# A decoder layer with a Mamba-2 mixer: B and C of a group in a turn of their own, by seven block products, and two products of out_proj over two turns

## The chip, the core and the metric

The kernel runs on one core of a Trainium2 chip. A core has a matrix engine (PE, with the loading of weights into its array shown as PEld), a vector engine (DVE), a scalar engine (ACT), GpSimd (POOL) and a sync engine (SP), which here issues the DMAs. The engines run side by side and each works through its own queue in order; they wait for one another by semaphores. All data of this kernel are fp32, and a matmul appears in the trace as two passes. The metric is the device time of one execution in microseconds, lower is better. Before the change it is 869.28 us, the median of three runs (869.14 to 869.52).

## The reference

The layer takes `x`, two batches of 256 tokens of width 512, through three residual blocks, each after a layer norm: a Mamba-2 mixer, a product with a context that is rounded to 8 bits (fake quantisation), and a feed-forward with soft-selected low-rank experts. The mixer takes nearly all of the time:

```python
proj = h @ in_proj_w.T                      # 512 -> 8192 gate + 8192 hidden + 1024 B + 1024 C + 128 dt
hBC  = silu(causal_conv(hBC, conv_w, conv_b))       # four taps along the tokens, per channel
hid, B, C = split(hBC)                      # 128 heads of 64; 8 groups, each with one B and one C of 128
M      = einsum('bcihn,bcjhn->bcijh', C, B) * L     # L: decays between tokens of a chunk of 128
Y_diag = einsum('bcijh,bcjhp->bcihp', M, hid * dt)
Y_off  = ...                                # what the second chunk takes over from the first
y   = Y_diag + Y_off + D * hid
yg  = y * silu(gate)
ygr = yg * rsqrt(mean(yg * yg over the 1024 channels of a group) + eps)
out = (ygr * gnorm_w) @ out_proj_w.T        # 8192 -> 512
```

## The kernel before

The tokens of both batches lie side by side, T = 512 columns; S = 256 is one batch. `hT` holds the normed input, 512 channels as KD = 4 blocks of 128 partitions, 512 tokens. The 8192 hidden channels make 64 *tiles* of 128, and NG = 8 *groups* of GJ = 8 tiles. A tile needs 128 rows of `in_proj_w` for the hidden part and 128 for the gate.

**Seven products for eight.** The first nine tiles are projected plainly (`project`, L304): for hidden and gate four matmuls of 512 columns each, 8 in all. From tile 9 on the two row blocks (hidden, gate) and the two halves of the 512 input channels make a 2 x 2 block matrix, which meets the 2 x 2 blocks of `hT` (halves of the channels, batches). Seven products of two matmuls of 256 columns (`multiply`, L308), 14 in all, replace the plain eight of 512. For this POOL makes four sums of weights per tile (`sum_weights`, L358, tile `ws`; those of the input, `hs`, are made once). The first four products are in `begin` (L370), three more in `complete` (L399); DVE makes the sums between them (`sum_begun`, L389: L395 to L397; `sum_complete`, L406: L410, L411), with a first copy by ACT (L387). The result lies in the two PSUM banks of `xy`, of which there are two sets. The gate comes out negated, one batch of it in the SBUF tile `u`.

**B and C of a group** are projected plainly: `project_b` (L438) writes the PSUM bank `po` and `project_c` (L441) the bank `misc` (for group 1, `po`), four matmuls of 512 columns each (16 passes together). Each then gets the convolution (`Conv`, L315): the first tap on ACT (L322), three more on DVE (L329), SiLU on ACT (L340).

**A turn** of the main loop (L965) handles tile c = 8 g + j, and at the same time tile c-1 (convolution, gate, decays) and tile c-2 (the products of the state space). The queues of PE, DVE, ACT and POOL hold the instructions in just the order in which they are written; SP's order is set by a planner. On PE a turn is: `begin` of tile c; a product of out_proj; `heads` of tile c-2 (L511, bank `py`); in turn j = 3 the B of the next group; four transposes of tile c-1 (`by_tokens`, L477, `pht` in the bank `misc`, read by DVE into `hc`, L486); `complete` of tile c; in turn 3 the C of the next group (in group 0, C of group 1 in turn 4). In turn 6 and 7 the small products of B and C (`pcb`, `pcr`) stand behind `begin`.
On DVE a turn is: `sum_complete` of tile c-1 (which waits for PE's last product of the turn before); at times the end of a group's norm; in turn 1 of four groups the rounding of a block of the context (L281, L282); the first scan of decays (L498); the three taps; `sum_begun` of tile c; the second scan; the sums of out_proj; the gating of tile c-2 (L530, L533); `hc` of tile c-1. On POOL: the four weight sums of the next tile, the product of decays and B-C for each scan (L508, `mT`), the sums for out_proj, and the running sum of squares (L539, `sqsum`).

**out_proj of a group** runs while the next group is projected, again as seven block products, m1, m2, m6, m5, m7, m3, m4 in this order (`seventh`, L656), each eight matmuls (16 passes) into the one bank `po`. They stand in turns 1, 2, 4, 5, 6, 7 of the next group and turn 0 of the one after; turn 3 has none, since it holds B and C. The sums that these need are made on POOL (L592 to L623: s1 and s3 of a pair of tiles, s2, s4, and t1 to t4 of the weights `wo`). m2 is followed by the group's norm (`norm`, L542): `pss` on PE from `sqsum`, `var` on DVE, a power on POOL (`r_g`), and at the head of the next turn on DVE four small operations for the reciprocal root and two adds into `acc` (L652), which free `po`. The last group but one uses the order 1, 2, 5, 6, 7, 3, 4 in turns 1 to 7, and the last group a plain out_proj at the end.

Tile c+1's weights (two DMAs of 256 KB) and decays (two of 384 KB) are loaded in turn c; `wo` (two of 1 MB per group) in turn 1 by the program, earlier by the planner, into three buffers.

Of the kernel before, what the change touches and what calls it, by code (L numbers as in the profile page):

```python
# [54 lines left out]
def kernel(  # L55
# [34 lines left out]
    loaded = []  # L90

    def load_w(*rows, name):

        w = wpool.tile([P, 2, KD, P], F32, tag="w", name=name)
        if rows[1] == rows[0] + 1:
            ins = nc.sync.dma_start(out=w[:], in_=in_w[rows[0] : rows[0] + 2].rearrange("r p k o -> p r k o"))
        else:
            for n, r in enumerate(rows):
                ins = nc.sync.dma_start(out=w[:, n], in_=in_w[r])
        loaded.append(ins)  # L100
        return w

# [14 lines left out]
    cb = const.tile([P, 80], F32, name="cb")  # L117
    gw = const.tile([P, NG * GJ], F32, name="gw")
# [196 lines left out]
    class Conv:  # L315
# [3 lines left out]
        def __init__(self, dst, pv, c, name):  # L319
            self.dst, self.pv, self.c = dst, pv, c  # L320
            self.a = pool.tile([P, T], F32, tag="conv", name=f"conv_{name}")
            nc.scalar.activation(  # L322
                by_batch(self.a[:]), pv, AF.Identity, bias=cb[:, c : c + 1], scale=cw[:, c, 3:4]
            )

        def taps(self):
            av, pv, c = by_batch(self.a[:]), self.pv, self.c
            for d in range(1, 4):
                nc.vector.scalar_tensor_tensor(  # L329
                    av[:, :, d:],  # L330
                    pv[:, :, : S - d],
                    cw[:, c, 3 - d : 4 - d],
                    av[:, :, d:],
                    ALU.mult,
                    ALU.add,
                )

        def finish(self):
            self.taps()
            nc.scalar.activation(self.dst, self.a[:], AF.Silu)  # L340

    class Tile:


        def __init__(self, c):
            self.c, self.plain = c, c <= GJ
            self.lT, self.mT = [], []

    def load_tile(c):
        z = Tile(c)  # L350

        z.w = wpool.tile([P, 2, KD, P], F32, tag="w", name=f"w_{c}")
        for n, r in enumerate((HID0 + c, GATE0 + c)):
            loaded.append(nc.sync.dma_start(out=z.w[:, n], in_=in_w[r]))
        z.dec = load_decays(c)
        return z

    def sum_weights(z):  # L358
        if not z.plain:
            a11, a12, a21, a22 = (z.w[:, r, h, :] for r in range(2) for h in (lo, hi))  # L360
            s = pool.tile([P, 3, KD // 2, P], F32, tag="ws", name=f"ws_{z.c}")
# [8 lines left out]
    def begin(z):  # L370

        z.xy = ps_proj.tile([P, 2, T], F32, tag="xy", name=f"xy_{z.c}")
        if z.plain:
            for n in range(2):
                project(z.xy[:, n, :], z.w[:, n])
            return
        z.halves = [z.xy[:, n, half] for n in range(2) for half in (slice(0, S), slice(S, T))]
# [6 lines left out]
    def copy_first(z):  # L384
        if not z.plain:
            z.u = pool.tile([P, 2, S], F32, tag="u", name=f"u_{z.c}")
            nc.scalar.copy(z.u[:, 0], z.halves[0])  # L387

    def sum_begun(z):  # L389
        if not z.plain:  # L390
            z.v = pool.tile([P, 2, S], F32, tag="v", name=f"v_{z.c}", bufs=1)
            _, x1, _, y1 = z.halves
            u0, u1 = z.u[:, 0], z.u[:, 1]
            y = z.xy[:, 1, :].rearrange("p (n s) -> p n s", n=2)
# [11 lines left out]
    def sum_complete(z):  # L406
        if not z.plain:
            x1 = z.halves[1]
            y = z.xy[:, 1, :].rearrange("p (n s) -> p n s", n=2)
            nc.vector.tensor_tensor(x1, x1, z.u[:, 0], ALU.add)  # L410
            nc.vector.tensor_tensor(y, y, z.v[:], ALU.add)  # L411

    def start_conv(z):
        z.hid = pool.tile([P, T], F32, tag="hid", name=f"hid_{z.c}", bufs=2)
        flat = z.xy[:].rearrange("p n s -> p (n s)")
        z.conv = Conv(z.hid[:], by_batch(flat[:, 0:T] if z.plain else flat[:, S : S + T]), z.c, f"h_{z.c}")

    def gates(z, half):
# [6 lines left out]
        elif half == 0:  # L425
            nc.scalar.activation(z.gate[:], z.xy[:, 1, :], AF.Silu)  # L426

    def load_bc(g):
        return load_w(B0 + g, C0 + g, name=f"wbc_{g}")

# [752 lines left out]
```

## Time and profile before

| | us |
|---|---|
| median of three runs | 869.28 (869.14 to 869.52) |
| the profiled execution | 869.89 |
| its span, first to last instruction | 867.0 |
| from the start of c in group 1 to that in group 2 | 98.87 |
| granted PE clock, mean over the span | 0.997 |

The page gives busy time per engine over the span. Matmul ends are modelled, so PE's share says little alone; the *chain* does more: it goes back from the last instruction, at each step to what released it, and lists start, length and engine with the line. A row of the *timeline* has start, length, engine, line, operation, output and inputs, shapes, count, and in brackets the idle time before it with what ended it. A row of the *windows* has the stretch, its length, then the busy time of PE, PEld, DVE, ACT and POOL (with counts), the PE clock, the DMA share and GB/s. Line numbers with L are those of the kernel before.

### The profile page before, as it was taken

What the parts mean: (1) busy time and instruction counts of PE and PEld (TensorE: products, weight loads), DVE (VectorE), ACT (ScalarE), POOL (GpSimd) and SP (SyncE); (2) the same over time, 40 slices, a digit from 0 to 9 for tenths busy, and PEclk for the clock granted to TensorE, in tenths of its full rate; (3) what the DMA queues carried; (4) which work ended last, traced back from release to release, by engine and by line L of the source; (5) the groups of instructions that cost most, each with busy time, mean ns of one, the idle gap of its engine ahead of it and who ended that gap; (6) DMA issues with size and microseconds to landing.
All of it is one profiled execution on the core that took longest, in us unless ns stands there. A gap on an engine that the chain in (4) does not pass through costs nothing.

```text
span 867.0 us, 12832 instructions
## 1 busy us (share of the span) xinstructions
PE 855.9 (99%) x4360; PEld 641.8 (74%) x4360; DVE 719.0 (83%) x1133; ACT 360.5 (42%) x779; POOL 631.2 (73%) x614
## 2 busy tenths in 40 slices
PE   8999999999999999999999999999999999999998
PEld 6444586888868886888868887788868888885453
DVE  5668798998898998988899888988799888995663
ACT  2444554444444443444444443444444443443220
POOL 2146798987799778987889778997789878973210
PEclk9999999999999999999999999999999999999998
DMA  6774453336433383336533362435333363323001
GB/s 171 221 268 146 140 169 114 112 109 225 141 106 131 109 254 117 106 120 203 169 105 122 104 219 89 133 108 177 140 119 112 111 209 104 122 86 122 0 1 48
DMA packets 54418, 116.19 MB, mean 134 GB/s; under 512 B 7217, under 2 KB 7473, under 8 KB 54354
## 3 DMA queue, kind: packets, MB, share of 16 engines
q1 hardware_dynamic: 54354, 115.39, 40.4%
q8 instruction: 34, 0.56, 0.3%
q14 instruction: 30, 0.25, 0.1%
HBM read 111.83 MB, written 3.54 MB: 133 GB/s over the span
## 4 chain that ended last, share of the span: by engine, by line
PE 85%; DVE 10%; DMA 1%; issue 1%; POOL 1%; ACT 1%; SPq 0%; ACTq 0%; POOLq 0%; DVEq 0%
PE xy L310 32%; PE m L643 18%; PE py L518 9%; PE xy L306 7%; PE pht L482 4%; PE c L306 3%; PE po L701 3%; DVE conv_h L329 2%; DVE lT L498 2%; PE pf L809 2%; PE pq L809 2%; PE pcb L451 1%; PE b L306 1%; DVE acc L652 1%; DMA wo<-in_out_w 1%
## 5 line engine op out<-in xcount | busy, mean ns | idle before, releaser
L508 POOL TENSOR_TENSOR mT<-lT,inner 128x768 f32<-128x768 f32 x128 | 233.4, 1824 | 128.6 <-ACT lT L502 115.6
L498 DVE TENSOR_TENSOR_SCAN lT<-dec,seed 128x512 f32<-128x512 f32 x128 | 154.9, 1211 | 0.0
L329 DVE SCALAR_TENSOR_TENSOR conv_h<-xy,cw,conv_h 128x510 f32<-128x510 f32 (+2 forms) x192 | 143.0, 745 | 13.7 <-ACT gate L426 5.5
L643 PE MATMUL m<-wo,yw 128*128 128x256 f32 x672 | 151.9, 379 | 0.0
L643 PEld LDWEIGHTS m<-wo,yw 128*128 128x128 f32 x672 | 126.8, 190 | 16.7
L502 ACT ACTIVATE lT<-dec,lT 128x128 f32<-128x128 f32 x256 | 88.8, 395 | 116.5 <-DVE lT L498 95.0
L310 PE MATMUL xy<-hT,w 128*128 128x256 f32 x440 | 113.8, 381 | 0.3
L310 PE MATMUL xy<-hs,w 128*128 128x256 f32 x440 | 112.9, 379 | 0.0
L310 PE MATMUL xy<-hs,ws 128*128 128x256 f32 x440 | 103.9, 379 | 0.0
L518 PE MATMUL py<-mT,hc 128*64 128x256 f32 (+1 forms) x1024 | 97.3, 332 | 0.0
L539 POOL TENSOR_TENSOR sqsum<-sqsum,sq 128x512 f32<-128x512 f32 x56 | 72.3, 1291 | 31.6 <-ACT sq L538 27.5
L518 PEld LDWEIGHTS py<-mT,hc 128*64 128x64 f32 x1024 | 63.4, 136 | 40.1 <-issue 16.1
L310 PEld LDWEIGHTS xy<-hs,w 128*128 128x128 f32 x440 | 83.6, 190 | 11.4
L310 PEld LDWEIGHTS xy<-hs,ws 128*128 128x128 f32 x440 | 83.6, 190 | 11.4
L310 PEld LDWEIGHTS xy<-hT,w 128*128 128x128 f32 x440 | 79.2, 190 | 13.0 <-DVE u L397 1.9
L538 ACT ACTIVATE sq<-y 128x512 f32<-128x512 f32 x56 | 35.3, 631 | 101.6 <-DVE y L533 97.3
L322 ACT ACTIVATE conv_h<-xy,cb,cw 128x512 f32<-128x512 f32 x64 | 49.6, 775 | 57.4 <-DVE xy L411 56.7
L530 DVE SCALAR_TENSOR_TENSOR py<-hid,dsk,py 128x512 f32<-128x512 f32 x64 | 47.8, 747 | 25.8 <-PE py L518 25.8
L306 PE MATMUL xy<-hT,w 128*128 128x512 f32 x144 | 63.3, 592 | 0.0
L310 PE MATMUL xy<-hT,ws 128*128 128x256 f32 x220 | 56.5, 379 | 0.0
L340 ACT ACTIVATE hid<-conv_h 128x512 f32<-128x512 f32 x64 | 40.4, 631 | 31.3 <-DVE conv_h L329 31.2
L410 DVE TENSOR_TENSOR xy<-xy,u 128x256 f32<-128x256 f32 x55 | 23.7, 431 | 35.3 <-PE xy L310 35.3
(205 smaller groups left out, 1341.6 us busy)
## 6 DMA issues: line engine op xcount, KB each, us to landing
dec<-decays SPq DMA_DIRECT2D x128, 384.0 KB, 3.4
w<-in_in_w SPq DMA_DIRECT2D x128, 256.0 KB, 3.1
wo<-in_out_w SPq DMA_DIRECT2D x16, 1024.0 KB, 8.0
wbc<-in_in_w SPq DMA_DIRECT2D x16, 256.0 KB, 3.9
kvin<-in_ctx_kv SPq DMA_DIRECT2D x4, 512.0 KB, 3.5
kvq<-kvin SPq DMA_DIRECT2D x4, 512.0 KB, 4.5
kv<-kvq SPq DMA_DIRECT2D x4, 512.0 KB, 3.6
acc<-in_x SPq DMA_DIRECT2D x4, 256.0 KB, 3.6
```

The source lines that it names most:

```text
L306: nc.tensor.matmul(pp, w[:, k, :], hT[:, k, :], start=(k == 0), stop=(k == KD - 1))
L310: nc.tensor.matmul(out, w[:, k, :], h[:, k, :], start=(k == 0), stop=(k == KD // 2 - 1))
L322: nc.scalar.activation(by_batch(self.a[:]), pv, AF.Identity, bias=cb[:, c : c + 1], scale=cw[:, c, 3:4])
L329: nc.vector.scalar_tensor_tensor(av[:, :, d:], pv[:, :, : S - d], cw[:, c, 3 - d : 4 - d], av[:, :, d:], ALU.mult, ALU.add,)
L340: nc.scalar.activation(self.dst, self.a[:], AF.Silu)
L498: nc.vector.tensor_tensor_scan(lT[:, 0:NT, :].rearrange("p t i -> p (t i)"), dec[:, 0:T], seed[:], 0.0, ALU.mult, ALU.add)
L502: nc.scalar.mul(lT[:, NT + b, :], dec[:, T + b * P : T + (b + 1) * P], lT[:, 2 * b, P - 1 : P])
L508: nc.gpsimd.tensor_tensor(m[:], z.lT[n][:], inner[:], ALU.mult)
L518: nc.tensor.matmul(z.py[n * HD : (n + 1) * HD, b * S + s * P : (b + 1) * S], z.hc[:, 2 * b + s, n, :], z.mT[n][:, part, :], start=(s == 0) ...
L530: nc.vector.scalar_tensor_tensor(py[:], hid[:], dsk[:, c : c + 1], py[:], ALU.mult, ALU.add)
L539: nc.gpsimd.tensor_tensor(sqsum[:], sqsum[:], sq[:], ALU.add)
L643: nc.tensor.matmul(o.po[:, t, :], lhs[k][:, t * P : (t + 1) * P], rhs[k], start=(k == 0), stop=(k == GJ // 2 - 1))
```

## The change

A group now has nine turns. Turn 4 (`BC`) belongs to the B and C of the next group, as a `State` that passes through the same functions as a tile: `load`, `sum_weights`, `begin`, `sum_begun`, `complete`, `sum_complete`. From group 2 on it is projected by the seven products, so C comes out negated, half of it in `u`: its convolution takes negated weights (`ncw`, made once) and runs in two halves (`parts`), 6 DVE taps of 256 columns in place of 3 of 512. A State has no decays, scans, `mT`, `heads`, gating or transposes. B and C of group 0 stay plain in the first turn, B now in `misc` and C in `po`; those of group 1 stay plain, B in `xy` and C in `po`. The last group keeps eight turns.

The products of out_proj stand at turns 1, 2, 4, 5, 6, 7, 8. `block` became a generator that may stop between its two halves (8 passes each): m2 runs in turns 2 and 3, m4 in turn 8 and turn 0 of the next group. The norm's `pss`, `var` and power stand ahead of the product in turn 2, its end and the adds of m2 at the head of turn 4. In the last group all products run whole, in turns 1, 2, 3, 5, 6, 7, 8. `pcb` and `pcr` stand at turns 7 and 8, ACT's copies of them ahead of the turn's decays.

```diff
@@ -316,49 +304,49 @@
-        def __init__(self, dst, pv, c, name):
-            self.dst, self.pv, self.c = dst, pv, c
+        def __init__(self, dst, pvs, w, c, name):
+            self.dst, self.w = dst, w
             self.a = pool.tile([P, T], F32, tag="conv", name=f"conv_{name}")
-            nc.scalar.activation(
-                by_batch(self.a[:]), pv, AF.Identity, bias=cb[:, c : c + 1], scale=cw[:, c, 3:4]
-            )
-        def taps(self):
-            av, pv, c = by_batch(self.a[:]), self.pv, self.c
+            av, n = by_batch(self.a[:]), NB // len(pvs)
+            self.parts = [(av[:, i * n : (i + 1) * n], pv) for i, pv in enumerate(pvs)]
+            for a, pv in self.parts:
+                nc.scalar.activation(a, pv, AF.Identity, bias=cb[:, c : c + 1], scale=w[:, 3:4])
+        def finish(self):
             for d in range(1, 4):
-                nc.vector.scalar_tensor_tensor(
-                    av[:, :, d:],
-                    pv[:, :, : S - d],
-                    cw[:, c, 3 - d : 4 - d],
-                    av[:, :, d:],
-                    ALU.mult,
-                    ALU.add,
-                )
-        def finish(self):
-            self.taps()
+                for a, pv in self.parts:
+                    nc.vector.scalar_tensor_tensor(
+                        a[:, :, d:], pv[:, :, : S - d], self.w[:, 3 - d : 4 - d], a[:, :, d:], ALU.mult, ALU.add
+                    )
             nc.scalar.activation(self.dst, self.a[:], AF.Silu)
...
+            self.c, self.name, self.plain = c, f"{c}", c <= GJ
+            self.rows = HID0 + c, GATE0 + c
             self.lT, self.mT = [], []
-    def load_tile(c):
-        z = Tile(c)
-        z.w = wpool.tile([P, 2, KD, P], F32, tag="w", name=f"w_{c}")
-        for n, r in enumerate((HID0 + c, GATE0 + c)):
-            loaded.append(nc.sync.dma_start(out=z.w[:, n], in_=in_w[r]))
-        z.dec = load_decays(c)
-        return z
+    class State:
+        def __init__(self, g):
+            self.g, self.name, self.plain = g, f"bc_{g}", g <= 1
+            self.rows = B0 + g, C0 + g
+    def load(z):
+        z.w = wpool.tile([P, 2, KD, P], F32, tag="w", name=f"w_{z.name}")
+        for n, r in enumerate(z.rows):
+            nc.sync.dma_start(out=z.w[:, n], in_=in_w[r])
+        if isinstance(z, Tile):
+            z.dec = load_decays(z.c)
...
+        if isinstance(z, State) and z.plain:
+            c = ps_out.tile([P, T], F32, tag="po", name=f"c_{z.g}")
+            if z.g == 0:
+                b = ps_misc.tile([P, T], F32, tag="misc", name="b_0")
+                z.xy = [b[:], c[:]]
+            else:
+                xy = ps_proj.tile([P, 2, T], F32, tag="xy", name=f"b_{z.g}")
+                z.xy = [xy[:, 0, :], c[:]]
+        else:
+            xy = ps_proj.tile([P, 2, T], F32, tag="xy", name=f"xy_{z.name}")
+            z.xy = [xy[:, n, :] for n in range(2)]
+            z.flat = xy[:].rearrange("p n s -> p (n s)")
         if z.plain:
             for n in range(2):
-                project(z.xy[:, n, :], z.w[:, n])
+                project(z.xy[n], z.w[:, n])
             return
...
+    def hid_of(z):
+        return by_batch(z.xy[0] if z.plain else z.flat[:, S : S + T])
     def start_conv(z):
-        z.hid = pool.tile([P, T], F32, tag="hid", name=f"hid_{z.c}", bufs=2)
-        flat = z.xy[:].rearrange("p n s -> p (n s)")
-        z.conv = Conv(z.hid[:], by_batch(flat[:, 0:T] if z.plain else flat[:, S : S + T]), z.c, f"h_{z.c}")
+        if isinstance(z, Tile):
+            z.hid = pool.tile([P, T], F32, tag="hid", name=f"hid_{z.c}", bufs=2)
+            z.convs = [Conv(z.hid[:], [hid_of(z)], cw[:, z.c], z.c, f"h_{z.c}")]
+            return
+        g = z.g
+        z.sT = [pool.tile([P, T], F32, tag=f"{n}T", name=f"{n}T_{g}", bufs=1) for n in "bc"]
+        z.convs = [Conv(z.sT[0][:], [hid_of(z)], cw[:, 64 + g], 64 + g, f"b_{g}")]
+        if z.plain:
+            pvs, w = [by_batch(z.xy[1])], cw[:, 72 + g]
+        else:
+            pvs, w = [a.unsqueeze(1) for a in (z.halves[3], z.u[:, 1])], ncw[:, g]
+        z.convs.append(Conv(z.sT[1][:], pvs, w, 72 + g, f"c_{g}"))
...
-    turns_of_sums = [usual_sums] * (NG - 1)
-    def block(o, lhs, rhs, name):
+    last_sums = {n + (n >= 4): of for n, of in usual_sums.items()}
+    turns_of_sums = [usual_sums] * (NG - 2) + [last_sums]
+    def block(o, lhs, rhs, name, split):
         o.po = ps_out.tile([P, 2, S], F32, tag="po", name=f"{name}_{o.g}")
         for t in range(2):
+            if t == split:
+                yield
...
-    def seventh(o, m):
+    def seventh(o, m, split):
         sub, add = ALU.subtract, ALU.add
         early = o.g == NG - 2
+        split = 1 if split else None
         if m == 0:
-            block(o, left(o, 0, 0), right(o, 0, 0), "m1")
+            yield from block(o, left(o, 0, 0), right(o, 0, 0), "m1", split)
             o.u = pool.tile([P, 2, S], F32, tag="ou", name=f"ou_{o.g}", bufs=1)
             nc.scalar.copy(o.u[:], o.po[:])
         elif m == 1:
-            block(o, left(o, 0, 1), right(o, 1, 0), "m2")
-            middle, end = norm(o)
+            yield from block(o, left(o, 0, 1), right(o, 1, 0), "m2", split)
             nc.vector.tensor_tensor(o.po[:], o.po[:], o.u[:], add)
-            middle()
-            return lambda: (end(), add_block(o, 0, 0))
+            ends_of.append(lambda: (o.end_norm(), add_block(o, 0, 0)))
         elif m == 2:
...
-    usual = {1: 0, 2: 1, 4: 2, 5: 3, 6: 4, 7: 5, 8: 6}
-    turns = [usual] * (NG - 2) + [{1: 0, 2: 1, 3: 3, 4: 2, 5: 4, 6: 5, 7: 6}]
+    GT = GJ + 1
+    BC = GJ // 2
+    order = []
+    for g in range(NG):
+        for q in range(GT):
+            if q != BC:
+                order.append((g, q, Tile(g * GJ + q - (q > BC))))
+            elif g + 1 < NG:
+                order.append((g, q, State(g + 1)))
+    order += [(NG, q, None) for q in range(2)]
+    usual = {1: (0, 0), 2: (1, 1), 4: (2, 0), 5: (3, 0), 6: (4, 0), 7: (5, 0), 8: (6, 1)}
+    turns = [usual] * (NG - 2) + [{1: (0, 0), 2: (1, 0), 3: (3, 0), 5: (2, 0), 6: (4, 0), 7: (5, 0), 8: (6, 0)}]
+    going = []
     inner = {}
-    NTILE = NG * GJ
     last_o = outs[NG - 1]
+    def products_of_state(g, q):
+        if g < NG and q == GT - 2:
+            inner[g] = inside(g, *state.sT)
+        if g < NG and q == GT - 1:
+            between(g, *state.sT, inner[g], (ps_misc, "misc"))
...
+    for s, (g, q, z) in enumerate(order):
+        z1, z2 = (order[s - n][2] if s >= n else None for n in (1, 2))
+        tile1 = isinstance(z1, Tile)
+        c = g * GJ + q - (q > BC) if q != BC or g == NG else None
         if z:
             begin(z)
-        if c + 1 < NTILE:
-            tiles.append(load_tile(c + 1))
-            sum_weights(tiles[c + 1])
+        if order[min(s + 1, len(order) - 1)][2]:
+            load(order[s + 1][2])
+            sum_weights(order[s + 1][2])
...
+        if g > 0:
+            products_of_state(g + 1, q)
...
+        if q == 2 and 0 < g < NG:
+            middle, outs[g - 1].end_norm = norm(outs[g - 1])
+            middle()
...
+        if z1 and not tile1:
+            z1.convs[1].finish()
+            state = z1
+        for o, turn in ((outs[g] if g < NG else None, q - GT), (outs[g - 1], q)):
             if o and 0 <= o.g <= g and not o.plain:
                 for stage, n in turns_of_sums[o.g].get(turn, ()):
                     stage(o, n)
...
-        for o, turn in ((outs[g - 1], j), (outs[g - 2], j + GJ)):
-            if 0 <= o.g < g and not o.plain and turn in turns[o.g]:
-                ends_of.append(seventh(o, turns[o.g][turn]))
...
+        o = outs[g - 1]
+        if not going and 0 <= o.g < g and not o.plain and q in turns[o.g]:
+            going.append(seventh(o, *turns[o.g][q]))
+        if going and next(going[0], True):
+            going.pop()
...
+        if s == 0:
+            begin(state)
+            start_conv(state)
+            state.convs[0].finish()
```

## The prediction

> **What bounds the kernel now.** I read four views: the page's busy line, whole groups by windows, the chain, and PE's own timeline where the chain leaves PE. The busy line:
>
> ```profile
> PE 855.9 (99%) x4360; PEld 641.8 (74%) x4360; DVE 719.0 (83%) x1133; ACT 360.5 (42%) x779; POOL 631.2 (73%) x614
> ```
>
> PE's 99% is modelled and proves little; that the others are clearly below it is to be seen. Next, two whole groups (window, its length, then busy us of PE, PEld, DVE, ACT, POOL), cut at the start of `c`:
>
> ```profile
> 146.06:244.93 98.87, 98.46 (x533) 79.62 (x533) 88.11 (x132) 44.00 (x98) 82.87 (x82) 1.00 0.44 144
> ...
> 541.40:640.27 98.87, 98.46 (x532) 79.62 (x533) 86.38 (x130) 42.76 (x97) 82.19 (x82) 1.00 0.40 133
> ```
>
> The first holds the rounding of a context block, the second doesn't: DVE works 1.7 us less and the length stays. The chain in two stretches (start, us, what):
>
> ```profile
> 639.62 0.61 DVE hc L486
> 640.23 0.04 issue
> 640.27 3.70 PE c L306 x8
> 643.97 3.45 PE xy L310 x16
> 647.42 3.45 PE m L643 x16
> 650.88 1.48 PE py L518 x16
> 652.35 0.11 issue
> 652.46 0.63 PE pht L482 x4
> 653.09 6.04 PE xy L310 x28
> ...
> 724.44 2.61 PE xy L310 x12
> 727.05 0.02 issue
> 727.07 0.44 DVE xy L410
> ...
> 730.21 0.89 DVE acc L652 x2
> 731.10 0.14 issue
> 731.23 3.69 PE m L643 x16
> ```
>
> PE follows PE, except before `c` and, in the last group, before one out_proj product (731.23). PE's timeline of turn 3, where b and c lie:
>
> ```profile
> 236.21 1.52 PE L518 MATMUL py<-mT,hc 128*64 128x256 f32 x16
> 237.66 3.70 PE L306 MATMUL b<-hT,wbc 128*128 128x512 f32 x8
> 241.20 0.60 PE L482 MATMUL pht<-ident,hid 128*128 128x128 f32 x4
> 241.82 1.13 PE L310 MATMUL xy<-hT,w 128*128 128x256 f32 x4
> ...
> 244.93 1.55 PE L306 MATMUL c<-hT,wbc 128*128 128x512 f32 x3 [0.25 <-DVE hc L486]
> ```
>
> PE pieces of one group by the chain: eight tiles of 6.04 (28 passes of 256 columns, 0.2157 each), eight py of 1.45, eight pht of 0.59, seven out_proj products of 3.45, pcb 0.89, pcr 0.45, pss 0.79 and b with c, 16 passes of 512 columns. Such 16 take 6.87 where nothing interrupts (the plain tiles), 0.4294 each. Sum 97.85. The chain's period is 98.84 (541.43 to 640.27): 1.0 us per group is PE waiting, nearly all around b and c. So a steady group is bound by PE, with 10 us of room on DVE and 16 on POOL; only order within a turn can make PE wait.
>
> **The change, part by part.** Times below count from PE's start of a turn.
>
> *Block products.* The B and C of groups 2 to 7 go from 16 passes of 0.4294 (6.87) to 28 of 0.2157 (6.04): -0.83 in six groups, -5.0. Groups 0 and 1 stay plain. All of it is on the path.
>
> *Own turn.* With b and c gone from turn 3, the waits at 241.20 (for hid), 241.82 (for L397), 244.93 (the misc bank, still read by hc) and 652.35 have no instruction to hold: up to -1.0 in six groups. Bounds 0 to -6.0; I take -6.0, as the split turns below keep more distance.
>
> *The split products.* They cost PE nothing. They make turns of 9.8 (0), 11.5 (1), 10.6 (2), 9.8 (3), 11.5 (4, the states), 10.9 (5), 10.1 (6), 12.4 (7) and 10.3 (8). But m2 now ends in turn 3, so its rstd and add come at the head of turn 4 on DVE, and m6 of that turn needs the one `po` bank that this add frees. Before, turn 3 had the rstd and no product. The last group shows the very sequence: from 727.07 rstd and add end at 731.10, and the product that could start at 727.05 + 3.45 = 730.50 starts at 731.23. That is a new wait of 0.73, plus DVE's lateness at the start of turn 4. Bounds: 0.73, and 1.1 with DVE 0.4 late; I take 0.85, six times, +5.1. Behind it on PE wait m6, py, pht and the rest of the turn; DVE uses the time to finish that turn's sums, so nothing else is late.
>
> *DVE.* A tile's turn takes DVE 9.2 (turn 0 of the second group, 197.27: L486 issues at 207.58 and frees DVE 0.6 later, less 0.2 at the start and 1.5 for m4's adds). The state adds L395 to L397 (1.5) and L410, L411 (1.1) and six half taps for three whole ones. A half tap isn't in the trace: between 0.44 (L652, 256 columns, 24.5 us over 56) and 0.745 (L329 whole); I take 0.44, nearer in size. Turn 4 also gets rstd and add (2.9, 233.94 to 236.84) and m6's sum (0.65); turn 5 has neither scans nor hc, but a wait of 0.8 for ACT's first tap. Turns 0 to 8 by DVE: 10.7, 9.2, 9.3, 9.9, 12.7, 10.2, 10.0, 10.7, 9.2, sum 91.9 against PE's 97.0. sum_begun ends 6.2 after L410, and PE asks for it at 7.2 in half-product turns, 8.9 in full ones. So turn 0 hands on 0.9 of lateness, which turn 1 absorbs unless the rounding (1.94, 210.08 to 212.02) lies there: 0.2 + 0.9 + 1.9 + 6.2 = 9.2 against 8.95, +0.25 in groups 2 to 4, +0.75. (In group 1, turn 0 holds a plain tile and no product.) With taps of 0.745 turn 6 would begin 1.7 late and wait 0.5, +3 in all.
>
> *POOL.* Four weight sums more per group (0.73 each, L364 to L367), +2.9. The heavy pair is turns 2 and 3: 25 us of work in 20.4. By the rows of 221.88 to 247.6 laid end to end from 1.5 into turn 2: weight sums 2.95, mT 1.8, r_g 1.2, s1 and s3 1.5, t1 2.45, mT 1.75; then 2.95, 1.8, s2 2.75, t2 2.45, done at 23.4. m6 asks for the last at 20.4 + 3.45 + 0.86 = 24.7, and 0.85 later with its wait. 2.1 to spare: cost nothing; this cover is the first rival. pss moves ahead of m2, to 3.45 in turn 2, and waits for sqsum, which POOL frees at 1.5 (221.88 against 220.34): nothing.
>
> *ACT, queues.* ACT has some 50 us free per group; its pieces for C (256 columns, 0.37 to 0.48) stand before the taps as a gate's do now. SP: state weights are the same 16 loads, without decays, so that turn loads less. The wo load that m4 releases issues 6.3 into turn 0 (203.54) and would issue at 4.6; with the row's median landing of 8.0 it is there at 12.6, asked for at 14.1; at the worst landing, 9.8, 0.3 late. Nothing, as now.
>
> *Unchanged:* prologue, group 0, last group from turn 1, tail.
>
> *Sum:* -5.0 - 6.0 + 5.1 + 0.75 = -5.1. The profiled execution took 869.89, 0.6 above the median of 869.28; -5.1 gives 864.8 against it, **864.2** against the median.
>
> **Two rules weighed.** *A DVE operation with two SBUF inputs:* three of C's six taps read the SBUF half (u) and accumulate in SBUF. The one such row, L675, took 742 ns against 666 for L673 beside it, while the POOL pair L619 took 2.95 against 2.5: by it, +0.2 on DVE and up to +1.4 on POOL per group, in turn 5 where both have it; nothing on PE. The Trainium skill, "SBUF — State Buffer", section "Who interferes with whom", says that such an instruction contends with GpSimd reading SBUF, and that the one that issues first blocks the other. Taken fully, each of the three would sit out a POOL sum of 0.73, 2.2 per group on DVE, and PE would wait some 0.9 in turn 6, six times: about 869.5 as an estimate. This rule speaks against the change; L675 shows a tenth of it.
>
> *PE's headroom:* PE pieces adjoin in the chain although weight loads are busy 74%. The window without rounding is as long as the one with it, on 1.7 us less DVE. The Trainium skill, "Perfetto Trace Analysis", section "Identifying the Most-Contended Engine", judges PE by its arithmetic and the weight loads' busy share, not by matmul busy time; by the 74% PE would have room and DVE, at 83%, would be the engine to relieve, so that 0.83 less on PE would give nothing and 3.0 more on DVE would cost up to 18 in six groups. The window contradicts it here.
>
> **The rivals.**
> *Slower: POOL late for m6.* For: the pair of turns holds more POOL work than PE time, with no b and c to stretch turn 3 as now. Against: POOL even idles 2.2 before its mT of turn 3 now (238.86). Each us beyond the 2.1 costs six. It ends slower once POOL is 3 us later than laid out; at 3.5, 864.2 + 6 x 1.4 = 872.6.
> *No gain: DVE is late around the states.* C's half taps take 0.745 and PE waits 0.5 in turn 6 (867.2), or half a clash with POOL as in L282 (2182 ns once, 1098 else) comes on top and it waits 1.0 (870.2). For: DVE is fullest in turn 4. Against: no half-sized DVE row takes over 0.48.
> *More gain: m6 doesn't wait,* because DVE starts the sums earlier than PE needs the bank: 864.2 - 5.1 = 859.1. Against: the group-7 lines, where DVE started at once and it waited all the same.
>
> **How the numbers follow.** Forecast 0.68 (862 to 867.5, its own bounds: m6 at 0.73 and no late turn 1 below, half of the old waits staying above); DVE late 0.13; POOL late 0.12; m6 free 0.07. 0.2% is 1.7 us, about what a measurement can tell from no change. Faster (below 867.5): the forecast, m6 free and a third of "DVE late", 0.79; within 0.2%: the rest of it, 0.08, rounded down for a late turn elsewhere; slower: POOL late and that, 0.13. The range, 860 to 869.5, holds the forecast and most of "DVE late", not POOL late and little of m6 free.
>
> **What would show it.** b and c gone and new 28-pass groups in the chain at 0.2157; a period of 97.9 per group (98.2 with rounding); one PE wait per group of 0.7 to 1.1 before the product of turn 4, released by DVE's add; half taps of 0.44 spacing; POOL's t2 done before that product. Wrong if PE waits for POOL there, for L397 in turns 0, 1, 3 or 6, or if the period stays at 98.8.

## The result, and the profile after

The changed kernel takes 892.73 us (median of five, 892.03 to 893.29) where the kernel before took 869.14 beside it (869.08 to 869.52): ratio 1.0269, 95% interval 1.0254 to 1.0284. The forecast was 864.2, with a range to 869.5. The profiled execution has a span of 890.5 us against 867.0, and a mean granted PE clock of 0.984 against 0.997. Line numbers below are those of the changed kernel unless another is named.

The busy line of the page, and two whole groups cut from one m6 to the next (window, length, then busy us of PE, PEld, DVE, ACT, POOL, then the granted clock):

```profile
PE 862.4 (97%) x4432; PEld 662.8 (74%) x4432; DVE 754.7 (85%) x1182; ACT 366.0 (41%) x791; POOL 647.8 (73%) x638
...
253.14:356.14 103.00, 99.36 (x544) 82.88 (x545) 93.49 (x141) 44.94 (x98) 85.64 (x86) 0.98 0.42 138
562.73:663.35 100.62, 97.41 (x545) 81.71 (x545) 91.67 (x139) 43.58 (x97) 85.02 (x86) 1.00 0.39 131
```

These two groups are 4.1 and 1.8 us longer than the 98.87 of before, and PE is no longer busy throughout: 3.6 us idle in the first window, 3.2 in the second. In the first PE is also 2 us busier than in the second, at a clock of 0.98. The table of PE's waits says where it stood (us in total, times, longest):

```profile
PE m L643 <- DVE acc L652: 21.2, 7, 3.5
```

In the steady groups the table has one wait: m6 in turn 4, for the add that frees its bank (its other rows, 1.5 us and less, lie at the start and the end of the kernel). The wait of c for the misc bank (1.5 us in six times before) is gone, and none for hid or L397 is in it. The one of m6 is the wait that the prediction named, at 3.2 to 3.5 us in groups 1 to 6 instead of 0.85; the seventh (0.7) is that of the last group, which was there before. Turn 4 of group 1, engines mixed in order of time:

```profile
142.60 2.49 POOL L610 TENSOR_TENSOR wo<-wo,t 128x512 f32<-128x512 f32 x2
142.68 0.70 DVE L411 TENSOR_TENSOR xy<-xy,v 128x512 f32<-128x512 f32 x1
...
143.28 0.60 DVE L48 TENSOR_TENSOR t_g<-r_g 128x4 f32<-128x4 f32 x1
143.92 1.19 DVE L49 TENSOR_TENSOR t_g<-t_g,var 128x4 f32<-128x4 f32 x1
144.60 1.03 PE L298 MATMUL xy_bc<-hs,w_bc 128*128 128x256 f32 x4
145.05 1.80 POOL L503 TENSOR_TENSOR mT<-lT,inner 128x768 f32<-128x768 f32 x1
145.14 1.73 DVE L50 TENSOR_SCALAR t_g<-t_g 128x4 f32<-128x4 f32 x1
146.81 1.26 POOL L534 TENSOR_TENSOR sqsum<-sqsum,sq 128x512 f32<-128x512 f32 x1
146.91 1.18 DVE L51 TENSOR_TENSOR rstd<-r_g,t_g 128x4 f32<-128x4 f32 x1
148.02 0.72 POOL L352 TENSOR_TENSOR ws<-w 128x256 f32<-128x256 f32 x1
148.12 0.88 DVE L652 SCALAR_TENSOR_TENSOR acc<-m,rstd,acc 128x256 f32<-128x256 f32 x2
```

L48 to L51 are the end of the norm: four operations on 128x4 numbers. They take 4.8 us from the start of the first to the start of the add (143.28 to 148.12). In turn 3 of the kernel before it was 2.1 (233.94 to 236.05), beside POOL's weight sums:

```profile
233.77 0.73 POOL L364 TENSOR_TENSOR ws<-w 128x256 f32<-128x256 f32 x1
233.94 0.58 DVE L48 TENSOR_TENSOR t_g<-r_g 128x4 f32<-128x4 f32 x1
234.55 0.16 DVE L49 TENSOR_TENSOR t_g<-t_g,var 128x4 f32<-128x4 f32 x1
234.58 0.73 POOL L365 TENSOR_TENSOR ws<-ws,w 128x256 f32<-128x256 f32 x1
234.75 0.59 DVE L50 TENSOR_SCALAR t_g<-t_g 128x4 f32<-128x4 f32 x1
235.27 0.72 POOL L366 TENSOR_TENSOR w<-w 128x256 f32<-128x256 f32 x1
235.37 0.64 DVE L51 TENSOR_TENSOR rstd<-r_g,t_g 128x4 f32<-128x4 f32 x1
...
236.05 0.88 DVE L652 SCALAR_TENSOR_TENSOR acc<-m,rstd,acc 128x256 f32<-128x256 f32 x2
```

Back in turn 4 of the changed kernel, read the ends of DVE's rows beside the starts of POOL's: L49 ends at 145.11, POOL's product with the mask starts at 145.05; L50 ends at 146.87, the sum of squares starts at 146.81; L51 ends at 148.09, the weight sum starts at 148.02. By these rows each small operation lasts until POOL's running one is over; the rows of before fit as well (L48 ends at 234.52, POOL's sum at 234.50), and L49, which started 0.03 us ahead of POOL's next sum, took 0.16. PE was ready at 145.62 and started m6 at 149.14.

Then m6 itself is slow. First PE's timeline in groups 1 and 5 (in brackets the idle time before), then the windows from PE's stop on in group 1 (the clock is the third number from the right):

```profile
149.14 6.37 PE L643 MATMUL m<-wo,yw 128*128 128x256 f32 x16 [3.52 <-DVE acc L652]
...
562.73 3.69 PE L643 MATMUL m<-wo,yw 128*128 128x256 f32 x16 [3.24 <-DVE acc L652]
```

```profile
145.60:149.10 3.50, 0.02 (x1) 0.00 (x0) 3.43 (x5) 0.37 (x1) 3.42 (x4) 0.81 0.00 0
149.10:152.60 3.50, 3.46 (x8) 2.86 (x9) 3.43 (x5) 1.19 (x4) 3.16 (x4) 0.50 0.10 20
152.60:156.00 3.40, 3.40 (x15) 2.42 (x15) 2.75 (x5) 1.14 (x3) 3.15 (x4) 0.71 0.31 98
```

After the idle 3.5 us the clock stands at 0.50, and the 16 passes take 6.37 us instead of 3.69. In five of the six groups m6 takes 5.3 to 6.7 us; in group 5, after 3.24 us, it keeps its 3.69. The Trainium skill, "TensorE: Matmul & The Clock Gate", Part 1, has a rule for this: after an idle window of about 3.4 us the array runs at half its clock, and the window runs freely, so that it matters where an idle stretch falls in it. That the length alone does not decide is so here: 3.24 us left the clock as it was, 3.21 us in group 6 lowered it to 0.50. But those 3.21 us are already shorter than the page's window, and experiment 4 has a wait of 2.80 us that lowered the clock; the measurement decides.

### The profile page after: what moved, and what is told of

The parts are those of the page before. It is cut to its first block, busy times and chain, and to the rows that moved or that the text cites. A ratio compares the mean times of both kernels' runs of the same rounds, so it can differ in the third digit from the quotient of the medians.

```text
span 890.5 us, 13140 instructions
## 1 busy us (share of the span) xinstructions
PE 862.4 (97%) x4432; PEld 662.8 (74%) x4432; DVE 754.7 (85%) x1182; ACT 366.0 (41%) x791; POOL 647.8 (73%) x638
## 4 chain that ended last, share of the span: by engine, by line
PE 79%; DVE 17%; issue 2%; ACT 1%; DMA 1%; SPq 0%; ACTq 0%
PE xy L298 30%; PE m L643 17%; PE py L513 8%; PE xy L294 7%; DVE conv_h L318 3%; PE pht L477 3%; PE po L700 3%; DVE lT L493 2%; PE xy_bc L298 2%; PE pf L809 2%; PE pq L809 2%; DVE xy L411 1%; DVE t_g L50 1%; DVE v L396 1%; DVE acc L652 1%
## 5 line engine op out<-in xcount | busy, mean ns | idle before, releaser
L643 PE MATMUL m<-wo,yw 128*128 128x256 f32 x672 | 165.5, 399 | 20.6 <-DVE acc L652 20.6
L643 PEld LDWEIGHTS m<-wo,yw 128*128 128x128 f32 x672 | 133.1, 201 | 42.0 <-POOL ws L352 22.8
L298 PEld LDWEIGHTS xy<-hT,w 128*128 128x128 f32 x440 | 79.2, 190 | 10.9 <-DVE u L397 1.5
L294 PEld LDWEIGHTS xy<-hT,w 128*128 128x128 f32 x144 | 26.7, 190 | 30.4 <-issue 29.3
```

The lines of the kernel that those rows point to most:

```text
L294: nc.tensor.matmul(pp, w[:, k, :], hT[:, k, :], start=(k == 0), stop=(k == KD - 1))
L298: nc.tensor.matmul(out, w[:, k, :], h[:, k, :], start=(k == 0), stop=(k == KD // 2 - 1))
L643: nc.tensor.matmul(o.po[:, t, :], lhs[k][:, t * P : (t + 1) * P], rhs[k], start=(k == 0), stop=(k == GJ // 2 - 1))
```

## The experiments

Theory A: the norm's small operations are held up by POOL's running operations, m6 waits for them, and the waiting lowers the clock. Against it: B, DVE is merely late in turn 4; C, m6 waits for POOL's t2; D, m6 is slow for another reason than the clock. All edits are to the changed kernel unless said otherwise; line numbers shift by a few in each. The expectations write 5.3 and 2.3 us for what the rows above give as 4.8 and 2.1.

**1. The norm's end column by column.**

```diff
-            newton(nc, small, o.rstd[:], o.r0, var[:], NT, f"g{g}")
+            for i in range(NT):
+                r, v, t, k = (a[:, i : i + 1] for a in (o.r0, var, t0, o.rstd))
+                nc.vector.tensor_scalar(t, r, r, v, ALU.mult, ALU.mult)
+                nc.vector.tensor_scalar(t, t, -0.5, 1.5, ALU.mult, ALU.add)
+                nc.vector.tensor_scalar(k, r, t, None, ALU.mult)
```

> The four small operations that end the norm (128x4, two or one tensors from SBUF) become twelve of 128x1 in which one tensor and per-partition scalars are read; they stay where they are, on VectorE at the head of turn 4, ahead of the add that m6 waits for. In the changed kernel the four take 5.3 us instead of the 2.3 us of before, and each ends about 0.06 us after a GpSimd operation ends. Theory A (VectorE and GpSimd share a way to SBUF, and a small operation that reads two tensors waits until the running GpSimd operation is over): twelve at 0.155 us each, as the 128x1 rows in the tail, are 1.9 us; m6's wait falls from 3.5 us to about 0.1 to 0.3, m6 goes back from 5.3 to 3.45 us, and the time is 892.7 - 6 x 3.3 - 12 = about 861 us. Theory A in its wider form (any small operation of VectorE on SBUF waits, which the 1.73 us of the one-tensor row L50 speaks for): each of the twelve may wait for an operation of 0.7 to 1.8 us, the wait of m6 grows to 8 to 12 us, and the time to 920 to 945 us. Rival B (VectorE is merely late at the head of turn 4, and the long small rows are a sign of nothing): 3.4 us less of its own work at most as in A, or no change at all, 892 +- 2 us.

869.48 us (ratio to before 1.0009, 0.9999 to 1.0018), clock 0.999. From the timeline of DVE and POOL at the same place:

```profile
142.26 2.49 POOL L615 TENSOR_TENSOR wo<-wo,t 128x512 f32<-128x512 f32 x2
...
142.92 0.27 DVE L556 TENSOR_SCALAR t_g<-r_g,var 128x1 f32<-128x1 f32 x1
...
143.22 0.15 DVE L557 TENSOR_SCALAR t_g<-t_g 128x1 f32<-128x1 f32 x1
143.41 0.21 DVE L558 TENSOR_SCALAR rstd<-r_g,t_g 128x1 f32<-128x1 f32 x1
```

All twelve run at an even pace under POOL's operation: 0.26, 0.15 and 0.21 us at the median over 32 each, with hardly a spread. So neither the place nor DVE's lateness made the four long; B falls as the whole story, and so does the wider form of A. L557 is the operation of L50 on one column instead of four: 0.15 against 1.73. The time is 8.5 us above the 861 expected, since the wait did not vanish: m6 waits 1.14 or 1.15 us in five groups and 1.39 in group 2, where 0.1 to 0.3 were expected (the twelve cost 2.5 us, not 1.9, which is only a part of it). The clock kept up after these. The Trainium skill, "SBUF — State Buffer", section "Who interferes with whom", has both halves of it: a DVE instruction with two SBUF inputs contends with a GpSimd instruction that reads SBUF, one in a two-port mode (which `tensor_scalar` can enter) contends with GpSimd too, and whoever issues first blocks the other. That one column escapes, with the other factors given as scalars, is what these rows show.

**2. TensorE kept busy through the wait.** The S3 product of the state repeated four times, the same values into the same place. The first try stood behind DVE's reading of that place:

```diff
+        if q == BC and 0 < g < NG - 1:
+            for _ in range(4):
+                multiply(z.halves[3], z.s3, t3)
         if not going and 0 <= o.g < g and not o.plain and q in turns[o.g]:
```

> In turn 4 of groups 1 to 6, TensorE repeats the block product of S3 four more times (16 passes of 256 columns, 3.45 us, the same values into the same place) between the state's begun products and m6, that is in the 3.5 us in which it waits. The wait's cause is untouched. Theory A, clock part (m6 takes 5.3 to 6.7 us because the granted clock falls to 0.5 after 3.5 us of idling): the clock stays at 1.0, m6 takes 3.45 us in every group, the time falls by about 12 us to 880 to 882 us. Rival D (m6 is slow for another reason: its weight loads, VectorE reading its bank, POOL rewriting its operands beside it): m6 keeps 5.3 to 6.7 us, and the time stays at 892 to 894 us.

945.99 us (1.0889, 1.0872 to 1.0905): a test that missed. The repeats had to wait for DVE's last reading of what they overwrite, further down DVE's queue than the add:

```profile
PE xy_bc L298 <- DVE u_bc L397: 49.7, 6, 8.4
```

Six waits of up to 8.4 us tell nothing on m6. The second try puts the repeats directly behind the begun products:

```diff
         multiply(y1, z.s3, t3)
+        if isinstance(z, State):
+            for _ in range(4):
+                multiply(y1, z.s3, t3)
```

> Mends the first filler: the four repeats of the S3 product (3.45 us, the same values into the same place) now stand directly behind the state's begun products, ahead of VectorE's readings of that place and not behind them, in groups 1 to 6. TensorE then works through the 3.5 us in which it waits for the add. Theory A, clock part: the granted clock stays at 1.0, m6 takes 3.45 us in place of 5.3 to 6.7, and the time falls by about 12 us, 880 to 883 us, the add still ending at the same place. Rival D (m6 is slow for another reason than the clock): m6 keeps 5.3 to 6.7 us, 892 to 896 us.

881.37 us (1.0145, 1.0130 to 1.0160), span 879.6, clock 0.998. PE's timeline and the window of m6:

```profile
144.58 4.48 PE L298 MATMUL xy_bc<-hs,w_bc 128*128 128x256 f32 x20
149.17 3.69 PE L646 MATMUL m<-wo,yw 128*128 128x256 f32 x16
```

```profile
149.10:152.60 3.50, 3.43 (x16) 2.96 (x16) 3.43 (x5) 1.53 (x5) 3.17 (x4) 1.00 0.06 25
```

In group 1 m6 starts where it did (149.17 against 149.14), its small operations are as long as before (L49 to L51: 1.19, 1.74 and 1.18 at the median), and it runs at a clock of 1.00 in 3.69. D falls: the clock is worth 890.5 - 879.6 = 10.9 us.

**3. The same work on POOL in shorter operations.** The first half of theory A, tested from POOL's side: DVE's code is untouched.

```diff
-        nc.gpsimd.tensor_tensor(w[:, :, 0, 0:S], w[:, :, 1, S:D], o.t1[m][:], ALU.subtract)
+        for i in range(2):
+            nc.gpsimd.tensor_tensor(w[:, i, 0, 0:S], w[:, i, 1, S:D], o.t1[m][:, i], ALU.subtract)
```

Likewise the sum of squares in two halves and the product with the mask in three parts, for the one tile whose operations run there.

> The same work on VectorE and on GpSimd, but the GpSimd operations that run beside the norm's end (t2: two of 1.25 us; one product with the mask: 1.8 us; one sum of squares: 1.26 us) are cut into pieces of 128x256, about 0.7 us each. Theory A (a small VectorE operation on SBUF waits until the running GpSimd operation ends): each of the four then lasts at most about 0.7 us, 2.5 to 2.8 us together in place of 4.7 to 5.3; m6's wait falls from 3.5 to about 1.1 us, the clock stays, m6 takes 3.45 us, and the time is 892.7 - 6 x 2.4 - 12 = about 866 us (868 if the 0.9 us of more work per group on GpSimd make t2 late by 0.3). Rival B (VectorE is late because of its own work, or the long rows come from something other than the length of GpSimd's operations): the rows stay at 1.2 to 1.7 us, 892 us, or later by GpSimd's added 0.9 us, 893 to 898.

869.05 us (1.0001, 0.9992 to 1.0011), clock 0.998.

```profile
142.47 2.78 POOL L616 TENSOR_TENSOR wo<-wo,t 128x256 f32<-128x256 f32 x4
...
143.11 0.78 DVE L48 TENSOR_TENSOR t_g<-r_g 128x4 f32<-128x4 f32 x1
...
143.93 0.65 DVE L49 TENSOR_TENSOR t_g<-t_g,var 128x4 f32<-128x4 f32 x1
...
144.62 0.66 DVE L50 TENSOR_SCALAR t_g<-t_g 128x4 f32<-128x4 f32 x1
145.21 2.08 POOL L505 TENSOR_TENSOR mT<-lT,inner 128x256 f32<-128x256 f32 x3
145.31 0.64 DVE L51 TENSOR_TENSOR rstd<-r_g,t_g 128x4 f32<-128x4 f32 x1
```

POOL's operations went from 1.2 to 1.8 us down to 0.7, and DVE's, in which nothing was changed, from 1.2 to 1.7 down to 0.65. The length of the small rows follows the length of POOL's operations. m6 waits 1.2 to 1.6 us in groups 1 to 6, 8.6 in all, where 1.1 each were expected; these are 2 of the 3 us that the time lies over the 866.

**4. The splitting undone.** `usual` with (1, 0) in turn 2 and (6, 0) in turn 8: m2 and m4 whole, the add a turn ahead of m6.

> Undoes the splitting of the two out_proj products in groups 1 to 6: m2 whole in turn 2, m4 whole in turn 8; the state's turn and its seven block products stay. The norm's end and the add of the first block then stand at the head of turn 3, a whole turn before m6. Theory A (the 3.5 us are the small operations directly ahead of m6, and the rest is the clock after it): the small operations may stay as long as they are, m6's wait goes, its 16 passes take 3.45 us, and the time is 892.7 - 21 - 12 = about 860 us, up to 864 us if turns 2 and 8, fuller by 1.7 us of TensorE, get a wait of 0.3 us each. Rival B (turn 4 itself overloads VectorE and GpSimd, whoever stands ahead of m6): m6 or the next consumer still waits 2 to 3.5 us, 875 to 893 us.

896.94 us (1.0324, 1.0309 to 1.0339): worse than the change, and above B's range too. A's number fails, and B's wait appears in another turn. From the waits of PE and the timelines of DVE and PE in turn 3 of group 2:

```profile
PE pht L477 <- ACT hid L321: 23.0, 12, 3.5
```

```profile
238.31 0.74 DVE L48 TENSOR_TENSOR t_g<-r_g 128x4 f32<-128x4 f32 x1
...
240.57 0.88 DVE L652 SCALAR_TENSOR_TENSOR acc<-m,rstd,acc 128x256 f32<-128x256 f32 x2
...
242.49 2.29 DVE L318 SCALAR_TENSOR_TENSOR conv_h<-xy,cw,conv_h 128x510 f32<-128x510 f32 x3
...
245.56 1.11 PE L477 MATMUL pht<-ident,hid 128*128 128x128 f32 x4 [3.46 <-ACT hid L321]
```

m6's wait is gone, as A has it. But turn 3 now has neither b and c nor half a product, PE comes to `pht` 3.5 us early, and DVE's convolution stands behind the norm's end (2.3 with its gaps), the add and the scan. So the split has a use: it fills turn 3. Here the clock falls after all six of the long waits (2.80 to 3.47 us), in group 1 after the one of 2.80 us to 0.66 and 0.51 in the 2.7 and 1.6 us that follow, so 3.4 us is no safe limit.

**5. The norm's end on POOL.** Five operations of 128x4 behind the power in turn 2, groups 0 to 6:

```diff
             o.r0 = power(nc, small, var[:], NT, f"g{g}")
+                nc.gpsimd.tensor_tensor(t0[:], o.r0[:], o.r0[:], ALU.mult)
+                nc.gpsimd.tensor_tensor(t0[:], t0[:], var[:], ALU.mult)
+                nc.gpsimd.tensor_tensor(t0[:], t0[:], halves[:, 0], ALU.mult)
+                nc.gpsimd.tensor_tensor(t0[:], t0[:], halves[:, 1], ALU.add)
+                nc.gpsimd.tensor_tensor(o.rstd[:], o.r0[:], t0[:], ALU.mult)
```

> The norm's end of groups 0 to 6 goes to GpSimd: five operations of 128x4 straight behind the power in turn 2; at the head of turn 4 VectorE has only the add. Theory A: the add ends at about 144.2 us in group 1 where PE is ready for m6 at 145.6, so the wait on VectorE is 0, the clock stays, and the time is 892.7 - 21 - 12 = about 860 us, if the five operations take GpSimd 0.1 us each (its 128x4 fill takes 0.11) to 0.6 in all. Rival C (GpSimd is what m6 really waits for): the operation t2 ended 0.6 us before PE was ready for m6; if the five take up to 1.0 us each (the 128x4 power takes 1.02), t2 ends up to 5 us later, m6 then waits up to 4.4 us for GpSimd, and the time is 870 to 898 us. Rival B (VectorE late in any case): the wait on the add stays above 1 us.

860.04 us (0.9900, 0.9885 to 0.9914), clock 0.999: faster than both kernels. Each of the five takes 0.20 us on POOL. PE waits for no add any more. C is true in small: t2 now ends at 145.96, and the loading of m6's weights waits for it, 2.2 us in six times. A variant with four operations (DVE writes -var/2 beside var, straight from PSUM):

> The norm's end on GpSimd in four operations instead of five, VectorE making -var/2 beside var (one more operation of 0.15 us, straight from PSUM). In the version with five, m6 waits 2.2 us in all, six times, for t2 on GpSimd. Theory (GpSimd's queue ahead of t2 is what is left of m6's wait, one for one): t2 comes 0.28 us earlier in each group, 860.0 - 6 x 0.28 = 858.4 us. Rival (another wait takes its place, or the wait is not GpSimd's): 860.0 +- 0.5 us.

858.92 us (0.9884, 0.9869 to 0.9899), the fastest of all; the wait for t2 is down to 0.8. The two intervals overlap, so only the trace tells these two apart.

**6. What the seven products are worth.** The five-operation version with every state projected plainly (`self.plain` always true, the sixteen 512-column passes into both halves of `xy`).

> The kernel with the norm's end on GpSimd (860.0 us), and B and C of groups 2 to 7 projected plainly again, in a turn of their own: 32 passes of 512 columns... in time 16 x 0.4294 = 6.87 us in place of 28 x 0.2157 = 6.04, and no sums of the state's weights (4 x 0.73 us of GpSimd), no sums on VectorE. By the prediction's first term the seven products are worth 0.83 us per group: 860.0 + 5.0 = 865.0 us; 863 us if GpSimd's relief also takes away the 0.37 us per group in which m6 waits for t2. Rival: the seven products' added sums cost as much as they save, 860 +- 1 us; or the plain state's long begin leaves a neighbouring turn's consumer late, 868 us and more.

863.30 us (0.9933, 0.9916 to 0.9949); the text's 32 passes is a slip for 16. m6's wait for t2 is gone. Against the 860.04 of the same five operations (another chip) the seven products are worth 3.3 us, net of the 2.2 us of t2 that their weight sums bring; against the 858.92 of the four, from the same chip, where 0.8 of that wait is left, 4.4 us, 4.7 by the spans.

**7. The split undone, with the norm's end on POOL** (the version of 858.92, turns as in experiment 4).

> The kernel with the norm's end on GpSimd in four operations (858.9 us), with the splitting undone: m2 whole in turn 2, m4 whole in turn 8. Undoing it alone gave 896.9 us: in turn 3 TensorE, without a half product there, waited 2.8 to 3.5 us for VectorE's convolution of the tile (behind the norm's end, 2.2 us, and the add, 0.9 us), and 0.57 us in turn 0. Theory (the work ahead of the convolution on VectorE sets it): without the norm's 2.2 us the wait in turn 3 is 0.6 to 1.3 us, too short to lower the clock, and that of turn 0 stays: 858.9 + 6 x (1.0 + 0.6) = about 868 us. Rival E (the split is worth nothing once the norm's end is gone): 859 to 861 us. Rival F (turn 3 is short of TensorE's work whatever VectorE does): 885 to 897 us.

873.40 us (1.0052, 1.0037 to 1.0067).

```profile
PE pht L477 <- ACT hid L321: 10.5, 12, 1.2
```

Expected were 868, and no rival's range holds 873.4. In turn 3 the norm's end was 2.3 of the 3.5 us (1.18 are left in each group), and the waits in turns 3 and 0 come to 10.5 us, without a fall of the clock. 858.92 + 10.5 makes 869.4; the other 4 us stay unassigned. Between these two kernels the split is worth 14.5 us.

**8. The kernel before, with only the norm's end moved to POOL** (the same four operations, nothing of the change).

> The kernel before, with nothing of the change, but with the norm's end on GpSimd in four operations as in the 858.9 us version. There the add of the first block stands at the head of turn 3 and m6 comes a turn later, and the trace showed TensorE waiting for the add only once, 0.7 us, in the last group (which keeps VectorE's norm). If the gain of that version over the kernel before (10.4 us) is the change's own (seven products and the state's own turn), this gives 869 us, within 1 us. Rival (the norm's end on VectorE cost the kernel before as well, since it delays the convolution behind it): 860 to 866 us.

861.34 us (0.9914, 0.9897 to 0.9930). The rival holds, and it is the run that corrects me most. The wait in the last group, which the text gives to VectorE's norm, is gone as well: the norm ended there is that of group 6, which moved with the others. The add of turn 3, which had begun at 236.05 (1.2 us of the difference are the group's earlier start, 1.1 the shorter norm's end):

```profile
233.75 0.88 DVE L661 SCALAR_TENSOR_TENSOR acc<-m,rstd,acc 128x256 f32<-128x256 f32 x2 [0.90 <-POOL rstd L563]
```

and in PE's timeline nothing holds b, pht or c:

```profile
236.48 3.70 PE L306 MATMUL b<-hT,wbc 128*128 128x512 f32 x8
240.01 0.60 PE L482 MATMUL pht<-ident,hid 128*128 128x128 f32 x4
240.45 1.03 PE L310 MATMUL xy<-hT,w 128*128 128x256 f32 x4
...
243.04 3.60 PE L306 MATMUL c<-hT,wbc 128*128 128x512 f32 x8
```

Of the 10.4 us that the best version gained, 7.8 came from four tiny operations, and no part of the change was needed for them. The lengths of the groups, from the start of one pcb on PE to the next (the third to fifth, and the sixth and seventh; the rounding falls in the first three):

| | third to fifth | sixth, seventh | median us |
|---|---|---|---|
| before | 98.86, 98.84, 98.84 | 98.84, 98.83 | 869.14 |
| before, norm's end on POOL | 97.88, 97.89, 97.89 | 97.88, 97.89 | 861.34 |
| changed | 103.01, 102.90, 104.35 | 100.65, 102.21 | 892.73 |
| changed, plain states, norm's end on POOL | 98.38, 98.39, 98.39 | 97.99, 97.99 | 863.30 |
| changed, norm's end on POOL (four) | 97.62, 97.61, 97.63 | 97.17, 97.17 | 858.92 |
| the last, m2 and m4 whole | 99.85, 99.86, 99.86 | 99.85, 99.85 | 873.40 |

## Why the prediction was wrong, step by step

*PE bounds a steady group:* right. With the small operations out of the way the period is 97.89 for the old pieces, whose sum was 97.85 (as printed the pieces add up to 97.79), and 97.17 for the new, by the same sum 97.02.

*Block products, -5.0:* right. -0.77 and -0.82 per group (98.39 to 97.62, 97.99 to 97.17), 4.7 us by the spans.

*Own turn, -6.0:* the waits did go, but the reason was wrong. I gave them to b and c in turn 3. Experiment 8 leaves b and c there, takes the norm's end off DVE, and the 1.0 us per group is gone (span 867.0 to 859.3, -7.7). The small operations delayed what stood behind them on DVE. The own turn alone did not remove the wait in turn 3: with the norm's end left there (experiment 4) PE waited 2.8 to 3.5 us for hid; it went when the split carried the norm's end into turn 4. Own turn and split by themselves cost 861.9 - 859.3 = 2.6 us of span, 2.0 by the medians (863.30 against 861.34).

*The split products, +5.1: this is the step that failed.* The mechanism and the place were named: rstd and add on DVE ahead of m6. The size was 0.85 per wait, with bounds of 0.73 and 1.1, and it measured 3.2 to 3.5, 20.6 us in six. Both bounds came from rows of the same four operations beside POOL's weight sums, 0.72 us each (the last group's too, from 727.94 on); in turn 4 POOL runs its 1.2 to 1.8 us operations, and 2.7 us of growth on top of 0.85 is the 3.5 measured. The rows in hand said so: L49 took 0.16 and L50 0.59 in one place, though both handle 128x4 numbers, and a duration that depends on the neighbour can't be moved to other neighbours. The prediction weighed the rule of the Trainium skill that covers it ("SBUF — State Buffer", section "Who interferes with whom"), but only on C's half taps, where it is small (0.48 to 0.56 for the half in SBUF, 0.47 for that in PSUM, 0.44 taken). It called L675 the one row with two SBUF inputs; L48, L49 and L51 are such rows too, and they were the ones that mattered.

*No term for the clock:* missing altogether, 10.9 us. With a wait of 0.85 none was to be expected: after waits of 1.1 to 1.6 the mean clock was 0.998 and 0.999.

*Rounding turns, +0.25:* 0.44 (97.61 against 97.17); in the group from 276.02 of the four-operation version the loading of weights waits once for L397, 0.4 us, the wait that was named.

*POOL, 2.1 us to spare, cost nothing:* t2 ended only 0.5 us before PE was ready (145.09 against 145.62); it cost nothing in the changed kernel, but the five operations of 0.20 us made it show.

*The second rule:* the Trainium skill, "Perfetto Trace Analysis", section "Identifying the Most-Contended Engine", would have named DVE as the engine to relieve; I set that aside with "the window contradicts it". I was half wrong: less work on PE did pay (-4.7), as the page's measure would not have it, but relieving DVE at one place paid more (-7.7). A window that stays equally long with 1.7 us less DVE work in *another* turn says nothing on the work in turn 3.

*The rivals:* "m6 doesn't wait" gave 859.1, and once the cause was taken away the kernel took 860.04 and 858.92. That the numbers are so near is partly luck: the -6.0 in that sum was given to the wrong cause, and POOL had more to do in those runs. The slower rival named POOL, by a late t2; POOL was the cause, but by holding up DVE.

The sum, by spans: -7.7 (norm's end out of turn 3), +2.6 (own turn and split, the rounding with them), -4.7 (products), +20.6 (m6's waits), +10.9 (clock) make +21.7 of the +23.5; 1.8 us stay unassigned. The terms come from several chips, on which the kernel before differed by up to 0.5 us in the median.

## What to carry to other kernels

The duration of a small vector operation is no property of the operation alone: before moving one, look at what GpSimd runs at its new place, and price each at about the length of the operation beside it, as it came out here. A chain of tiny operations ahead of something the bounding engine waits for may be better placed elsewhere, here on GpSimd, which makes their input; moving four of them there was worth 7.8 us in the old kernel, and turns this change from a loss of 2.7% into a gain of 1.2%. Price a new wait on TensorE twice: once as idle time, and once, if it may near 3 us, as half speed after it (2.80 us was enough here, 1.6 was not).

## What the hardware showed that I had not expected

- A 128x4 operation of DVE in SBUF (0.16 or 0.17 us when left alone) lasts until POOL's running operation ends: 1.19, 1.73 and 1.18 beside 1.25, 1.80 and 1.26; 0.65 beside 0.7. It holds for one tensor and immediate numbers (L50) as for two tensors; on a 128x1 column that form of L50 took 0.15.
- PE's clock fell to 0.50 after five of six waits of 3.2 to 3.5 us (one of 3.21 among them), not after the one of 3.24, and in experiment 4 to 0.51 after one of 2.80.
- GpSimd does a 128x4 product in 0.20 us, where the power on the same numbers takes 1.02.
